# Block 0 of a retention and FFN layer: constants on another queue, and another order of copies, scan, variance products and weight sums

## The chip, the core and the metric

The kernel runs on one core of a Trainium2 chip. The metric is the device time in microseconds (us) from the start to the end of one execution. A core has five engines that run side by side: TensorE (PE, with its weight loads PEld), VectorE (DVE), ScalarE (ACT), GpSimd (POOL) and SyncE (SP). SP issues most transfers, ScalarE issues a few. Every engine works through its own instructions strictly in the order in which the program writes them, and waits at an instruction whose operands or whose buffer are not ready.

## What is computed

One layer of a small network over 4 sequences of 1024 tokens with 512 features, in float32:

```python
lam = clip(1 - 2**-beta, tiny, 1 - 1e-9)
def attn(x):                               # x: (4, 1024, 512), normalised
    q, v = heads(x @ Wq.T), heads(x @ Wv.T)          # 16 heads of 32
    ret = scan(v)                          # state = lam * state + v_t, along each sequence
    out = layernorm(q * ret) * gamma + beta_ln
    return (out * silu(x @ Wg.T)) @ Wo.T
def ffn(x):                                # weights rounded to float8_e4m3, kept in float32
    gate = silu((x @ r8(gate_w)) * gate_scale)       # 512 -> 1536
    return ((gate * ((x @ r8(up_w)) * up_scale)) @ r8(down_w)) * down_scale
x = x + norm(attn(norm(x)))                # norm: layernorm without weights, eps 1e-5
x = x + norm(ffn(norm(x)))
```

## The kernel before

**Tiles and blocks.** The 4096 tokens are cut into eight blocks of TB = 512 tokens, each of NS = 4 tiles of 128 tokens. Features lie in NC = 4 chunks of 128, the FFN's inner dimension in NI = 12 chunks. A `Retention` object does the attention part of a block, an `Ffn` object its FFN. In what follows, `a` is block 0, `b` block 1, `n` block 2, `f` the FFN of the running block, `l` that of the block before.

**The order of the work.** All instructions go through `InOrder`, so each engine executes them exactly as the program text calls them. There is no planner. Block 0's attention is written out by hand, mixed with the start of block 1's. Then a loop over t (blocks) and i (12 chunks of the FFN) follows: step i computes `f.gate(i)`, `f.up(i)` and `f.fuse(i)`, and `f.down(i - 2)`, and `if` lines place pieces of the next blocks between them. Step t = 0 also does block 1's attention and prepares block 2.

**The attention part.** Each tile is normalised (`norm_x`), transposed on TensorE (`turn_x`, into a PSUM bank) and copied out (`keep_x`) into the tile xnT. That tile exists once: block 1's copies have to wait until block 0's last product that reads it, `a.gate(3)`, is through. `v(c)`, `q(c)` and `gate(c)` are the products with the weights, per chunk of features. Their PSUM banks are named: two called "pf", two called "pa0" and "pa1", four called "pd0" to "pd3". `scan(c)` is the retention scan on VectorE and frees the bank of `v(c)`; `y_of(c)` is the product q * ret. `silu(c)` on ScalarE frees the bank of `gate(c)`. The normalisation of y goes over the features, that is over partitions: `mean` and `var` are products of a sum with a matrix of 1/512. `center_y` subtracts the mean and builds the squares' sum on ScalarE and POOL. `var` also issues the square root on ScalarE, whose functions need another table than silu's; `rstd_y` is the reciprocal of it on VectorE; `z(c)` scales y, applies gamma and beta and multiplies by the gate. In block 1, `halves` first splits a sum into two fp32r parts, on ScalarE and VectorE.

**The output part.** For each tile s: `o(s)` is the product with Wo, `o_moments(s)` its mean and rstd (statistics on VectorE, rstd on POOL), `x1_of(s)` normalises it on ScalarE and adds x on POOL, `x1_moments(s)` and `x1n_of(s)` normalise the sum. `turn_x1n(s)` transposes on TensorE. From block 1 on, `move_x1n(s)` does it instead with 32 x 32 transpositions on VectorE and five transfers through DRAM on SP. `upper_of(s)` on ScalarE and `rest_of(s)` on VectorE split the result into the two fp32r parts that the FFN's products read.

**Rounding of the FFN's weights.** Pieces of 128 x 1024 are loaded, and `rounds(n)` takes n steps of a generator on VectorE: a mask, an addition, a subtraction into the weight tile (which also frees a buffer, so that SP loads the next piece). `units()` issues two ScalarE operations for each open mask.

**Weight sums.** Blocks 2 to 7 compute v, q and g by seven products of half-sized matrices in place of eight. `weight_sums(k)` makes the sums of the quarters of a weight matrix in place with four VectorE operations of 128 x 512; `keep_sums` stores the four results in DRAM (four transfers on SP). In the loop at t = 0 this is done for v, q and g at i = 8, 9 and 10: the sums right before `f.gate(i)`, after `b.x1_moments(i - 8)`, the stores near the end of the step. `fetch_weights` loads a factor into the ring `w_ring`, which takes the place of Wv, four at i = 9. `t_sums` takes that of Wq and `mids` that of Wg, so their first writers wait for the stores of the sums. `n.product()` at i = 11 begins block 2's products: it copies the first result to `mids` on ScalarE, behind `b.upper_of(2)`.

**The start.** `load_x` sends half of each of block 0's tiles by SP and half by ScalarE. Then `load_const` issues the six constants on ScalarE's queue, and `load_square` the weights on SP's. Ahead of all of ScalarE's computing stands one Exp on a constant, which loads its table.

Of the kernel before, what the change touches and what calls it, by code (L numbers as in the profile page):

```python
# [23 lines left out]
def retention_ffn_sandwich(  # L24
# [64 lines left out]

    def load_const(src, cols, name):  # L90
        t = const.tile([P, cols], F32, tag=name, name=name)
        act.dma_start(t, src)
        return t
# [7 lines left out]

    beta_sb = load_const(beta, NC, "beta_sb")
    wv_sb = load_square(wvT, "wv_sb")
    wq_sb = load_square(wqT, "wq_sb")
    gamma_sb = load_const(gamma, NC, "gamma_sb")
    lnb_sb = load_const(lnb, NC, "lnb_sb")
    gs_sb = load_const(gate_s, NI, "gs_sb")
    us_sb = load_const(up_s, NI, "us_sb")
    ds_sb = load_const(down_s.to_broadcast([P, D]), D, "ds_sb")

# [104 lines left out]
    def units():  # L215

        while open_units:
            _, c = open_units.pop(0)
            act.activation(c, c, AF.Relu, bias=neg_low)
            act.activation(c, c, AF.Identity, scale=1.5 * 2.0**20, bias=low_unit)  # L220
# [123 lines left out]

    def weight_sums(k):

        src, w = squares[k]
        v = src.rearrange("(c p) f -> p c f", p=P)
        a11, a12, a21, a22 = (w[:, i : i + 2, o : o + H] for o in (0, H) for i in (0, 2))
        operands[k] = {1: v[:, 0:2, 0:H], 2: v[:, 2:4, 0:H], 4: v[:, 2:4, H:D]}  # L350
        dve.tensor_tensor(a22, a21, a22, ALU.add)
        dve.tensor_tensor(a21, a11, a21, ALU.subtract)
        dve.tensor_tensor(a11, a22, a11, ALU.subtract)
        dve.tensor_tensor(a12, a12, a11, ALU.subtract)
        return {5: a22, 7: a21, 6: a11, 3: a12}

    def keep_sums(k, done):
        for j, t in done.items():
            operands[k][j] = dram.tile([P, 2, H], F32, tag=f"sum_{k}{j}", name=f"dsum_{k}{j}", bufs=1)
            sp.dma_start(operands[k][j], t)  # L360
# [482 lines left out]
    wg_sb = load_square(wgT, "wg_sb")  # L843
    squares["g"] = wgT, wg_sb
    a = Retention(0, x_first)
    a.new_xnT()
# [57 lines left out]
    for s in range(NS):  # L904
        b.turn_x(s, f"pd{s}")
    a.var()
    a.rstd_y()
    a.silu(2)
# [4 lines left out]
    b.keep_x(3, dve.tensor_copy)  # L913
    a.silu(3)
    units()
    b.v(0, "pf", early)
    b.v(0, "pf", later)
    for c in range(NC):
        a.z(c)
    b.v(1, "pf")  # L920
    b.scan(0)
    b.v(2)
# [40 lines left out]
    a.rest_of(2)  # L963
    rounds(3, now=False)
    a.turn_x1n(3)
    a.upper_of(3)
    b.q(2, "pd0", early)
    units()
    a.rest_of(3)
    b.y_of(1)  # L970

# [4 lines left out]
    for t in range(NB):  # L976
        f, n = Ffn(a), None
        fast = b is not None and b.fast
        for i in range(NI):
# [29 lines left out]
            if b and not fast and i == 5:  # L1009
                b.z(0)  # L1010
            if b and i >= 8:
                b.x1_moments(i - 8)
            if t == 0 and 8 <= i < 11:
                done = weight_sums("vqg"[i - 8])
            f.gate(i)
# [31 lines left out]
            if b and not fast and i == 4:  # L1047
                b.halves()
                rounds(3, now=False)
                b.g_of(1)  # L1050
                b.var()
            if b and not fast and i == 5:
# [20 lines left out]
            units()  # L1073
            f.up(i)
            f.fuse(i)
            if t == 0 and i == 4:
# [55 lines left out]
            if b and n and i == 11:  # L1132
                b.rest_of(3)
            if t == 0 and 8 <= i < 11:
                keep_sums("vqg"[i - 8], done)

# [28 lines left out]
            if t == 0 and i == 9:  # L1165
                w_ring = wpool.tile([P, RING, 2, H], F32, tag="wv_sb", name="w_ring")
                for _ in range(RING):
                    fetch_weights()
# [78 lines left out]
```

## Time and profile before

| what | value |
|---|---|
| median of three runs | 985.41 us (984.66 to 985.66) |
| the profiled execution | 985.64 us, of it the span of the profile 983.8 us |
| from the start to the first FFN product | 95.2 us |
| from the start to the first FFN product of t = 1 | 204.6 us |
| TensorE busy, 0 to 98 us | 94.05 us |
| TensorE busy, 98 to 205 us | 102.23 us |
| TensorE busy, 205 to 984 us | 768.65 us |
| VectorE busy in the same stretches | 75.61, 86.58, 501.51 us |

The table divides the span at the start of block 0's FFN and at the start of t = 1. All edits lie in code that runs before 205 us. In the profile, each instruction stands under its engine with the tiles that it writes and reads: pv, pq, pg, po, pfg, pfu and pd are the products of v, q, gate, o and of the FFN; ptx and pt are transpositions, scr the pieces of weights, st and mv statistics, xs the transposed tile on its way to DRAM (mxs). Behind an instruction stands, in square brackets, how long its engine was idle before it and what ended the wait. SPq and ACTq are issues of transfers.

### The profile page before, as it was taken

The numbers are of one execution on the slowest core, as the hardware profiler recorded it, in microseconds if no ns is written. First come the engines' busy times: TensorE is split into PE (matmuls) and PEld (weight loads), VectorE is DVE, ScalarE is ACT, GpSimd is POOL, SyncE is SP. The second block draws the span as 40 slices with busy tenths as digits, with TensorE's granted clock in tenths as the row PEclk, the third lists the DMA queues.
The fourth block names the chain that finished last, engine by engine and source line by source line (L and its number), as shares of the span: only waits on it lengthen the run. The fifth ranks groups of instructions, "written<-read, shape, count | busy, mean of one in ns | idle before, by whom it ended". The sixth has DMA issues, their size and how long they took to land.

```text
span 983.8 us, 11259 instructions
## 1 busy us (share of the span) xinstructions
PE 964.9 (98%) x3950; PEld 735.9 (75%) x3950; DVE 663.7 (67%) x1019; ACT 369.6 (38%) x556; POOL 265.7 (27%) x346
## 2 busy tenths in 40 slices
PE   9999999999999999999999999999999999999996
PEld 7455766678876888678876788768887788867885
DVE  5996979656666567665686666766667765656535
ACT  3555565466645125221432215321152211522323
POOL 1405121422324033240513305133142312322020
PEclk9999999999999999999999999999999999999998
DMA  9311323752416426254242623245241552213021
GB/s 296 122 62 65 130 65 90 213 178 76 150 53 152 127 77 234 77 139 127 86 129 88 180 75 115 89 131 151 83 150 59 134 139 78 73 43 107 1 86 43
DMA packets 90936, 110.07 MB, mean 112 GB/s; under 512 B 8064, under 2 KB 55424, under 8 KB 90880
## 3 DMA queue, kind: packets, MB, share of 16 engines
q1 hardware_dynamic: 89296, 108.43, 36.9%
q10 hardware_dynamic: 1584, 0.94, 0.4%
q8 instruction: 31, 0.51, 0.2%
q14 instruction: 25, 0.20, 0.1%
HBM read 76.56 MB, written 32.77 MB: 111 GB/s over the span
## 4 chain that ended last, share of the span: by engine, by line
PE 82%; DVE 9%; ACT 4%; POOL 2%; issue 1%; DMA 1%; SPq 0%; ACTq 0%; DVEq 0%; POOLq 0%
PE pfu L74 15%; PE pfg L74 15%; PE pd L74 15%; PE pv L74 10%; PE pq L74 9%; PE pg L74 9%; PE po L74 8%; DVE st L74 2%; DVE scr L74 1%; POOL mv L74 1%; POOL x L74 1%; DVE fuse L74 1%; ACT x1n L74 1%; DVE gate L74 1%; DVE xs L74 1%
## 5 line engine op out<-in xcount | busy, mean ns | idle before, releaser
L74 PE MATMUL pfu<-x1nT,up_sb 128*128 128x512 f32 x768 | 212.5, 419 | 0.0
L74 PE MATMUL pfg<-x1nT,gate_sb 128*128 128x512 f32 x768 | 195.3, 396 | 0.4 <-DVE x1nT L74 0.4
L74 PE MATMUL pd<-down_sb,fuse 128*128 128x512 f32 x720 | 186.8, 401 | 0.0
L74 PEld LDWEIGHTS pfu<-x1nT,up_sb 128*128 128x128 f32 x768 | 145.1, 189 | 42.5 <-issue 12.9
L74 PEld LDWEIGHTS pfg<-x1nT,gate_sb 128*128 128x128 f32 x768 | 144.2, 188 | 30.4 <-DVE x1nT L74 0.8
L74 PEld LDWEIGHTS pd<-down_sb,fuse 128*128 128x128 f32 x720 | 135.3, 189 | 27.5
L74 ACT CAST fuse<-gate 128x512 fp32r<-128x512 f32 x90 | 55.7, 619 | 235.5 <-DVE gate L74 235.5
L74 ACT ACTIVATE gate<-pfg,gs_sb 128x512 f32<-128x512 f32 x96 | 65.7, 684 | 195.6 <-PE pfg L74 195.5
L74 DVE SCALAR_TENSOR_TENSOR gate<-pfu,us_sb,gate 128x512 f32<-128x512 f32 x96 | 71.8, 748 | 73.7 <-PE pfu L74 71.2
L74 PE MATMUL po<-wo_sb,y 128*128 128x512 f32 x256 | 114.5, 592 | 0.0
L74 POOL TENSOR_SCALAR mv<-mv 128x1 f32<-128x1 f32 (+1 forms) x82 | 19.4, 237 | 300.3 <-DVE mv L74 299.2
L74 PEld LDWEIGHTS po<-wo_sb,y 128*128 128x128 f32 x256 | 48.2, 189 | 50.3 <-issue 46.6
L74 DVE TENSOR_TENSOR fuse<-gate,fuse 128x512 fp32r<-128x512 f32 x90 | 75.0, 834 | 12.4 <-ACT fuse L74 12.4
L74 POOL TENSOR_TENSOR ysum<-y 128x256 f32<-128x256 f32 (+1 forms) x14 | 14.0, 998 | 190.3 <-DVE y L74 190.3
L74 POOL TENSOR_TENSOR x<-x,x1n 128x512 f32<-128x512 f32 x32 | 46.8, 1462 | 45.7 <-DVE x1n L74 36.7
L74 DVE BATCH_NORM_STATS2 st<-x 128x6 f32<-128x512 f32 x64 | 43.6, 681 | 13.8 <-POOL x L74 11.2
L74 POOL TENSOR_TENSOR mv<-mv,nhalf 128x1 f32<-128x1 f32 (+1 forms) x75 | 46.1, 615 | 6.2
L74 PE MATMUL pg<-t_sums,w_ring 128*128 128x256 f32 x192 | 45.7, 381 | 0.6 <-ACT mids L74 0.6
L74 PE MATMUL pv<-t_sums,w_ring 128*128 128x256 f32 x192 | 45.3, 379 | 0.0
L74 PE MATMUL pq<-t_sums,w_ring 128*128 128x256 f32 x192 | 45.3, 379 | 0.0
L74 PEld LDWEIGHTS pg<-t_sums,w_ring 128*128 128x128 f32 x192 | 35.9, 189 | 7.3 <-ACT mids L74 2.1
L74 PEld LDWEIGHTS pv<-t_sums,w_ring 128*128 128x128 f32 x192 | 36.3, 189 | 5.7
(150 smaller groups left out, 1336.8 us busy)
## 6 DMA issues: line engine op xcount, KB each, us to landing
kept<-x SPq DMA_DIRECT2D x32, 256.0 KB, 2.1
x<-kept SPq DMA_DIRECT2D x32, 256.0 KB, 3.7
x<-in_x SPq DMA_DIRECT2D x28, 256.0 KB, 4.3
out<-d SPq DMA_DIRECT2D x27, 256.0 KB, 2.1
xnT<-mx SPq DMA_DIRECT2D x24, 256.0 KB, 4.8
w_ring<-dsum_v SPq DMA_DIRECT2D x24, 256.0 KB, 2.7
w_ring<-dsum_q SPq DMA_DIRECT2D x24, 256.0 KB, 2.7
w_ring<-dsum_g SPq DMA_DIRECT2D x24, 256.0 KB, 2.6
```

Source lines behind the costliest of these rows:

```text
L74: return lambda *args, **kwargs: tc.keep_in_program_order(op(*args, **kwargs))
```

## The change

The diff has six parts.

1. The constants gamma, lnb, gs, us and ds are loaded on SP's queue after Wg, in place of ScalarE's queue at the start; beta stays on ScalarE's.
2. In block 0, `a.var()` and `a.rstd_y()` follow the copies `b.keep_x` and `a.silu(3)` in place of preceding `a.silu(2)`. `b.scan(0)` precedes `a.z` and `b.v(1)`.
3. Of the three rounding steps before `a.turn_x1n(3)`, the third moves behind `a.rest_of(3)`.
4. At i = 4, `b.var()` follows `f.up(4)` in place of `b.g_of(1)`.
5. The weight sums become a generator: four steps for v at i = 8, six at i = 9 (q's four and two of g), two at i = 10, these ahead of `b.x1_moments(2)`. g's stores follow them at once; v's and q's stay where they were.
6. Of the first four loads into the ring, two are issued at i = 9 and two at i = 10.

```diff
--- before.py
+++ after.py
@@ -87,9 +87,9 @@
 
     x_first = [load_x(0, s, [sp, act]) for s in range(NS)]
 
-    def load_const(src, cols, name):
+    def load_const(src, cols, name, queue=None):
         t = const.tile([P, cols], F32, tag=name, name=name)
-        act.dma_start(t, src)
+        (queue or sp).dma_start(t, src)
         return t
 
     def load_square(src, name):
@@ -99,14 +99,9 @@
             sp.dma_start(w[:, 2 * h : 2 * h + 2, :], v[:, 2 * h : 2 * h + 2, :])
         return w
 
-    beta_sb = load_const(beta, NC, "beta_sb")
+    beta_sb = load_const(beta, NC, "beta_sb", act)
     wv_sb = load_square(wvT, "wv_sb")
     wq_sb = load_square(wqT, "wq_sb")
-    gamma_sb = load_const(gamma, NC, "gamma_sb")
-    lnb_sb = load_const(lnb, NC, "lnb_sb")
-    gs_sb = load_const(gate_s, NI, "gs_sb")
-    us_sb = load_const(up_s, NI, "us_sb")
-    ds_sb = load_const(down_s.to_broadcast([P, D]), D, "ds_sb")
 
 
     gate_sb = wpool.tile([P, NC, I], F32R, tag="gate_sb", name="gate_sb")
@@ -342,20 +337,28 @@
     squares = {"v": (wvT, wv_sb), "q": (wqT, wq_sb)}
     operands = {}
 
-    def weight_sums(k):
-
-        src, w = squares[k]
-        v = src.rearrange("(c p) f -> p c f", p=P)
-        a11, a12, a21, a22 = (w[:, i : i + 2, o : o + H] for o in (0, H) for i in (0, 2))
-        operands[k] = {1: v[:, 0:2, 0:H], 2: v[:, 2:4, 0:H], 4: v[:, 2:4, H:D]}
-        dve.tensor_tensor(a22, a21, a22, ALU.add)
-        dve.tensor_tensor(a21, a11, a21, ALU.subtract)
-        dve.tensor_tensor(a11, a22, a11, ALU.subtract)
-        dve.tensor_tensor(a12, a12, a11, ALU.subtract)
-        return {5: a22, 7: a21, 6: a11, 3: a12}
-
-    def keep_sums(k, done):
-        for j, t in done.items():
+    def weight_sums():
+
+
+        for k, (src, w) in squares.items():
+            v = src.rearrange("(c p) f -> p c f", p=P)
+            a11, a12, a21, a22 = (w[:, i : i + 2, o : o + H] for o in (0, H) for i in (0, 2))
+            operands[k] = {1: v[:, 0:2, 0:H], 2: v[:, 2:4, 0:H], 4: v[:, 2:4, H:D]}
+            made[k] = {5: a22, 7: a21, 6: a11, 3: a12}
+            dve.tensor_tensor(a22, a21, a22, ALU.add)
+            yield
+            dve.tensor_tensor(a21, a11, a21, ALU.subtract)
+            yield
+            dve.tensor_tensor(a11, a22, a11, ALU.subtract)
+            yield
+            dve.tensor_tensor(a12, a12, a11, ALU.subtract)
+            yield
+
+    made = {}
+    adding = weight_sums()
+
+    def keep_sums(k):
+        for j, t in made[k].items():
             operands[k][j] = dram.tile([P, 2, H], F32, tag=f"sum_{k}{j}", name=f"dsum_{k}{j}", bufs=1)
             sp.dma_start(operands[k][j], t)
 
@@ -842,6 +845,11 @@
         load_piece(n)
     wg_sb = load_square(wgT, "wg_sb")
     squares["g"] = wgT, wg_sb
+    gamma_sb = load_const(gamma, NC, "gamma_sb")
+    lnb_sb = load_const(lnb, NC, "lnb_sb")
+    gs_sb = load_const(gate_s, NI, "gs_sb")
+    us_sb = load_const(up_s, NI, "us_sb")
+    ds_sb = load_const(down_s.to_broadcast([P, D]), D, "ds_sb")
     a = Retention(0, x_first)
     a.new_xnT()
     warm(14)
@@ -903,8 +911,6 @@
     b.new_xnT()
     for s in range(NS):
         b.turn_x(s, f"pd{s}")
-    a.var()
-    a.rstd_y()
     a.silu(2)
     a.gate(3, "pf")
     b.keep_x(0)
@@ -912,13 +918,15 @@
     b.keep_x(2, dve.tensor_copy)
     b.keep_x(3, dve.tensor_copy)
     a.silu(3)
+    a.var()
+    a.rstd_y()
     units()
     b.v(0, "pf", early)
     b.v(0, "pf", later)
+    b.scan(0)
     for c in range(NC):
         a.z(c)
     b.v(1, "pf")
-    b.scan(0)
     b.v(2)
     b.scan(1)
     rounds(3)
@@ -961,12 +969,13 @@
     a.rest_of(1)
     b.y_of(0)
     a.rest_of(2)
-    rounds(3, now=False)
+    rounds(2, now=False)
     a.turn_x1n(3)
     a.upper_of(3)
     b.q(2, "pd0", early)
     units()
     a.rest_of(3)
+    rounds(1, now=False)
     b.y_of(1)
 
 
@@ -1008,10 +1017,15 @@
                 n.shift()
             if b and not fast and i == 5:
                 b.z(0)
+            if t == 0 and i == 10:
+                for _ in range(2):
+                    next(adding)
+                keep_sums("g")
             if b and i >= 8:
                 b.x1_moments(i - 8)
-            if t == 0 and 8 <= i < 11:
-                done = weight_sums("vqg"[i - 8])
+            if t == 0 and i in (8, 9):
+                for _ in range(4 if i == 8 else 6):
+                    next(adding)
             f.gate(i)
             if t == 0 and i in (5, 6):
                 n.norm_x(2 * i - 10, True)
@@ -1048,7 +1062,6 @@
                 b.halves()
                 rounds(3, now=False)
                 b.g_of(1)
-                b.var()
             if b and not fast and i == 5:
                 b.g_of(2)
                 b.z(1)
@@ -1072,6 +1085,8 @@
                 n.input_sums(1, 2, 3, 4)
             units()
             f.up(i)
+            if t == 0 and i == 4:
+                b.var()
             f.fuse(i)
             if t == 0 and i == 4:
                 b.rstd_y()
@@ -1131,8 +1146,8 @@
                 n.fetch_x()
             if b and n and i == 11:
                 b.rest_of(3)
-            if t == 0 and 8 <= i < 11:
-                keep_sums("vqg"[i - 8], done)
+            if t == 0 and i in (8, 9):
+                keep_sums("vq"[i - 8])
 
             if i == f.lag:
                 f.sums()
@@ -1164,7 +1179,8 @@
                 n.stats(1)
             if t == 0 and i == 9:
                 w_ring = wpool.tile([P, RING, 2, H], F32, tag="wv_sb", name="w_ring")
-                for _ in range(RING):
+            if t == 0 and i in (9, 10):
+                for _ in range(RING // 2):
                     fetch_weights()
             if t == 0 and i == 10:
                 t_sums = wpool.tile([P, 4, 2, H], F32, tag="wq_sb", name="t_sums")
```

## The prediction, made before the changed kernel was run

> **What bounds the kernel now.** I read the page first, then TensorE's waits, then the chain of waits, then the engine timelines of the stretches that the diff touches. All times are microseconds from the start of the profiled execution, whose span is 983.8 of 985.64.
>
> ```profile
> PE 964.9 (98%) x3950; PEld 735.9 (75%) x3950; DVE 663.7 (67%) x1019; ACT 369.6 (38%) x556; POOL 265.7 (27%) x346
> ```
>
> TensorE is busy 98% of the span, so a change is worth at most what TensorE waits in the stretch it touches. Who it waits for up to 250 us:
>
> ```profile
> PE pt L74 <- ACT x1n L74: 2.3, 2, 2.0
> PE pv L74 <- ACT xnT L74: 2.3, 2, 1.2
> PE var L74 <- ACT half L74: 1.4, 1, 1.4
> PE pv L74 <- ACT mids L74: 1.1, 1, 1.1
> ...
> PE pfg L74 <- DVE x1nT L74: 0.4, 1, 0.4
> ```
>
> Columns are the total, the count and the longest. After 205 us there is only 0.8 us of such waits in 779 us, so a shift at the end of block 0 is the shift of the whole kernel. Each wait above has an edit on it: the two on xnT (at 9.95 and 56.97), the one on x1nT (96.19), var (130.43), and turn and mids (197.64, 202.97). If TensorE were all that counted, they would all be gains. The timelines say otherwise. VectorE (DVE) has no idle of note from 42.9 to 74.2, and what follows is a chain of single steps:
>
> ```profile
> 54.12 3.35 DVE L74 RECIPROCAL rstd<-rstd 128x512 f32<-128x512 f32 x1
> 57.38 1.22 DVE L74 COPY xnT<-ptx 128x512 f32<-128x512 f32 x2
> ...
> 74.46 0.70 DVE L74 BATCH_NORM_STATS2 st<-po 128x6 f32<-128x512 f32 x1 [0.28 <-PE po L74]
> ```
>
> The reader is to see that at 74.46, where o_moments(0) starts, VectorE has 0.28 us of slack. From there the chain of waits goes statistics, POOL, ScalarE, POOL's addition, four times at 3.38 us per tile (POOL's additions start at 78.38, 81.77, 85.16, 88.55), and ends in the transposition of tile 3 at 93.21, for which TensorE waits. A later start at 74.46 is a later FFN. ScalarE (ACT) just before:
>
> ```profile
> 50.22 1.28 ACT L74 ACT_TABLE_LOAD   x1
> 52.41 0.69 ACT L74 ACTIVATE rstd<-var,eps_sb 128x512 f32<-128x512 f32 x1 [0.91 <-PE var L74]
> 53.11 1.28 ACT L74 ACT_TABLE_LOAD   x1
> 54.41 0.60 ACT L74 ACTIVATE g<-pg 128x512 f32<-128x512 f32 x1
> 55.84 1.07 ACT L74 COPY xnT<-ptx 128x512 f32<-128x512 f32 x2 [0.84 <-PE pg L74]
> ```
>
> Now the root is ready at 53.1, before VectorE wants it at 54.12: the reciprocal runs while TensorE does gate(3) (to 54.96) and b's copies wait for it, since both blocks share the tile xnT.
>
> **What the Trainium skill says.** ScalarE: Activation LUTs, "What ACT_TABLE_LOAD costs", gives about 1283 ns for a load, and its section on table sets says that cheap functions lie in every set; the trace agrees (1.28 us, and no load between the root at 132.19 and the Relu after it). DMA: Bandwidth & Descriptors, "Issuing engines are not separate DMA queues": moving an issue saves the sequencer's time alone; here five issues take 0.33 + 0.44 + 0.33 + 0.33 + 0.44 = 1.9 us of ScalarE's queue. GPSIMD Engine Reference, "Key points": POOL shares its SBUF interfaces with VectorE; beside the weights' additions POOL's two steps of a rstd take 0.54 + 1.00 us (186.26), alone 0.19 + 0.55 (195.59). TensorE: Matmul & The Clock Gate, Part 1: after an idle window the clock is halved for a window of about 3.4 us; the trace shows 0.50 granted in 132 to 134, after the wait for var.
>
> **Part 1, constants.** ScalarE's queue is held by its issues until 7.41, then come the table load (7.44), lam (8.74) and the copies (8.85 to 9.90); TensorE waits until 9.95. With beta alone on it the queue is free at 3.9 and the load ends near 5.2, so the copies follow the transpositions: the second ends at 8.41, its copy near 9.0, TensorE starts at 9.05. Gain 0.9; at least 0.5, if the second half of wv, issued at 5.7 and landing 3.7 to 4.4 later, is late for the fifth product. SP issues the five after wg, ahead of b's x (needed at 37.6) and wo (needed at 71): some 2 us of SP's queue, covered by over 15 us. wq no longer stands behind them. TensorE has no gap from 9.95 to 55.8, and VectorE follows it, so both carry the 0.9.
>
> **Part 2, var after the copies.** In the times of before: gate(3) ends at 54.96; ScalarE copies tiles 0 and 1 until 56.07, VectorE 2 and 3 until 56.15. The var product fills 54.96 to 55.8, so b.v(0) starts at 56.1 instead of 56.97: TensorE gains 0.8. But the root now stands behind silu(3) (to 56.6) and a table load (to 57.9) and ends at 58.55. VectorE waits from 54.2 to 54.96 and from 56.15 to 58.55, 3.2 us that it did not wait before. Behind the reciprocal stand all its work: scan(0) 1.4, z 5.9, scan(1) 1.4, rounds 3.0, scan(2), rounds and scan(3) 3.9. It reaches o_moments(0) at about 77.5 instead of 74.46: +3.0, bounds 2.0 and 3.6 (the root waits less, or the copies longer). The scan put first frees the bank for b.v(3) in time, so no further wait comes of it. TensorE's 0.8 is lost in front of turn(0): o(3) ends earlier, x1n comes later.
>
> **Part 3, rounds 2 + 1.** rest_of(3) waited for an addition and a subtraction until 95.45; now it follows upper_of(3), 94.5 to 95.1, before TensorE ends q(2) at 95.24. The first FFN group effectively began at 95.96 (seven products from 96.19, one of 0.23 done), so the gain is 0.7. VectorE is no earlier, but it has 0.33 and 1.02 us of waiting for pfu (101.74, 108.81), which take up the difference. Shift at 109: −0.9 + 3.0 − 0.7 = +1.4.
>
> **Part 4, b.var after up(4).** TensorE no longer waits 1.4 us, and may escape the halved window. But the root again goes behind: after silu g at 130.9, units() waits for the mask of 131.6 and holds ScalarE until 133.95, the table load until 135.2, the root until 135.95. The reciprocal starts at 136.0 instead of 135.40: +0.6 (bounds 0 and +1). The chain of waits runs through that reciprocal: scr, rest(4), the load at 142.36, silu(5), scr, VectorE at 148.48, then VectorE without idle to 170. z(3) ends at 155.73 and TensorE reaches o(0) at 156.35, so TensorE's gain ends in waits for silu(5) and y.
>
> **Part 5, additions.**
>
> ```profile
> 176.78 2.83 DVE L74 TENSOR_TENSOR wq_sb<-wq_sb 128x512 f32<-128x512 f32 x4
> 179.79 0.71 DVE L74 STREAM_TRANSPOSE xs<-x1n 128x512 f32<-128x512 f32 x1 [0.17 <-ACT x1n L74]
> ...
> 185.26 0.69 DVE L74 BATCH_NORM_STATS2 st<-x 128x6 f32<-128x512 f32 x1 [1.35 <-POOL x L74]
> ```
>
> Six of 0.71 instead of four at i=9: the transposition slips by 1.3. At i=10 two (1.4 us) stand ahead of the statistics, in idle time of 1.35, and POOL's rstd behind them runs alone: −0.8. x1n(3), which TensorE awaits at 197.64, comes +0.5 (to +1.1 if POOL's addition is slowed). On SP, dsum_g's four issues (2.9 us) now stand before the transposed tile's:
>
> ```profile
> 191.16 1.88 SPq L74 DMA_DIRECT2D mxs<-xs  x4
> 195.52 0.34 SPq L74 DMA_DIRECT2D x1n<-mxs  x1
> ```
>
> These go to about 194.2 and 198.6, upper_of(2) on ScalarE from 198.35 to 201.4, and behind it stand the cast of fuse and the copy to mids, at 202.45. Now that copy waits for dsum_g until 202.33. One wait replaces the other: +0.1 at 202.97, bounds −0.7 and +0.8. Two ring loads a step later are in time (j=2 lands near 202, needed at 203).
>
> **Sum.** −0.9 + 3.0 − 0.7 + 0.6 + 0.1 = +2.1 us; 985.64 + 2.1 = 987.7. The profiled execution lies 0.23 over the median of the runs, 985.41, so this is 0.23% over that median. A measurement of this kernel can tell about 0.2% from no change: 983.4 to 987.4.
>
> **Rivals.** Forecast, reciprocal's delay carried through, 987.7: for it VectorE's missing idle; against it that 0.3 us less is already within the bound. Chance 0.50, of it 0.35 slower and 0.15 same; its own range 986.4 to 989.0.
> A clock window on top: new waits in front of turn(0) (2.4 us) and at silu(5) halve the clock once, 1.7 us lost as at 132 to 135: 989.4. Against it, 2.05 us of waiting at 197 brought none. 0.17, slower.
> Slack takes up the delay, the other side: the one mechanism is the x1 chain of 74 to 93, which would have to run below 3.38 us per tile with its po ready early. Then 3.0 falls to 0: 985.64 − 0.9 = 984.7. It decides once it recovers over 0.4 of the 3.0. Against it, POOL's fixed order. 0.22, of it 0.20 same and 0.02 faster.
> TensorE's gaps are the bound after all: 0.9 + 0.8 + 0.7 + 3.1 (var and the halved window) + 0.7 (mids) = 6.2, 979.4. Against it, the chain of waits on other engines. 0.11, of it 0.09 faster and 0.02 same.
> Faster 0.11, same 0.37, slower 0.52. Range 984.0 to 990.3: it holds the first three and leaves out the last and the worst of the second.
>
> **What would show it.** TensorE's first v at 9.0; a reciprocal at about 57.6 with over 2 us of VectorE idle before it; o_moments(0) near 76.6; TensorE waiting over 2 us at turn(0); FFN about 97; VectorE waiting for the root at i=4; SP's mxs after dsum_g. Wrong if o_moments(0) isn't later, or if the root ends by 56.

## The result

| | median | runs | ratio to before, 95% interval |
|---|---|---|---|
| before | 985.39 us | 6, 984.66 to 985.68 | |
| after | 989.76 us | 6, 987.88 to 990.83 | 1.0043 [1.003, 1.0056] |

The changed kernel is 4.4 us slower. The sign and the range of the prediction held; its size, +2.1 us, is half of what was measured, and the forecast's own range, 986.4 to 989.0, was missed by 0.8. Three of the executions that follow were slow ones (1095.82 to 2035.05 us) and are left out of every median. The profiled execution of after took 990.15 us, of it a span of 988.3 us, 4.5 us more than that of before. The page of after, engines and their busy time:

```profile
PE 968.1 (98%) x3950; PEld 737.0 (75%) x3950; DVE 663.7 (67%) x1019; ACT 369.7 (37%) x556; POOL 264.7 (27%) x346
```

The work is the same: the counts are equal, and VectorE's busy time is 663.7 us in both. TensorE's busy time rose by 3.2 us with no product added, so something slowed its clock; more on that below. TensorE's waits up to 260 us in after (waited for by whom, total, times, longest):

```profile
PE pt L74 <- ACT x1n L74: 4.8, 3, 2.4
PE pfg L74 <- ACT gate L74: 2.7, 1, 2.7
...
PE pv L74 <- ACT xnT L74: 0.5, 2, 0.3
PE mu L74 <- DVE half L74: 0.5, 1, 0.5
PE pv L74 <- DMA wv_sb<-in_wvT: 0.4, 1, 0.4
```

Against before, the waits for xnT fell from 2.3 to 0.5, and those for half at var (1.4) and mids in front of pv (1.1) are gone. In their place stand 2.7 us for silu(5), which writes the gate, 2.5 more for x1n, 0.5 for half at mu, and 0.4 for the second half of wv. Of the waits that the edits were laid against, only the one for x1n has not gone or shrunk, and the kernel is slower.

Where the time came from shows in the start of the same instruction in both profiled executions:

| step | before | after | difference |
|---|---|---|---|
| o_moments(0) on VectorE | 74.46 | 76.69 | +2.23 |
| first FFN group (before: its effective start, as in the prediction) | 95.96 | 97.89 | +1.93 |
| reciprocal of b, i = 4 | 135.40 | 138.60 | +3.20 |
| first o of b | 156.35 | 160.01 | +3.66 |
| statistics of x(0), i = 8 | 166.65 | 170.28 | +3.63 |
| statistics of x(2), i = 10 | 185.26 | 190.82 | +5.56 |
| transposition of x1n(3) | 197.64 | 202.38 | +4.74 |
| first FFN product of t = 1 | 204.62 | 209.50 | +4.88 |

So the first 76 us lose 2.2, the FFN's pieces up to the reciprocal another 1.3, and the way of the last tiles, from i = 8 to the transposition, about 1.1. Each column is one execution, and two of them can differ at such a point without any edit: in the five kernels whose code is that of before up to o_moments(0), it starts between 74.12 and 74.91. First the stretch in which the prediction put the largest term. VectorE in after (start, duration, instruction, idle before it and what ended it):

```profile
54.46 1.29 DVE L74 COPY xnT<-ptx 128x512 f32<-128x512 f32 x2 [0.77 <-PE pg L74]
58.07 3.35 DVE L74 RECIPROCAL rstd<-rstd 128x512 f32<-128x512 f32 x1 [2.32 <-ACT rstd L74]
...
76.69 0.69 DVE L74 BATCH_NORM_STATS2 st<-po 128x6 f32<-128x512 f32 x1
```

and ScalarE in front of that reciprocal, in after:

```profile
54.46 1.07 ACT L74 COPY xnT<-ptx 128x512 f32<-128x512 f32 x2 [4.30 <-PE pg L74]
55.42 0.61 ACT L74 ACTIVATE g<-pg 128x512 f32<-128x512 f32 x1
56.06 1.28 ACT L74 ACT_TABLE_LOAD   x1
57.35 0.69 ACT L74 ACTIVATE rstd<-var,eps_sb 128x512 f32<-128x512 f32 x1
```

VectorE stands idle for 0.77 + 2.32 us where it had no idle before, because copy, silu, table load and root now lie in one row on ScalarE in front of its reciprocal. From there to 76.69 VectorE has no idle, so nothing takes the delay up.

At i = 4 the same pattern recurs. ScalarE in after:

```profile
134.22 1.15 ACT L74 ACTIVATE scr<-scr,neg_low 128x1024 f32<-128x1024 f32 x1 [0.87 <-DVE scr L74]
135.41 1.16 ACT L74 ACTIVATE scr<-scr,low_unit 128x1024 f32<-128x1024 f32 x1
136.58 1.28 ACT L74 ACT_TABLE_LOAD   x1
137.88 0.69 ACT L74 ACTIVATE rstd<-var,eps_sb 128x512 f32<-128x512 f32 x1
```

The root waits behind the two steps of a piece of weights, which in turn waited 0.87 us for VectorE's mask; the reciprocal at 138.60 then waits 1.35 us for the root. And the clock that TensorE was granted, by stretches of after (stretch, length, busy us and instructions of PE, PEld, DVE, ACT, POOL, granted clock, share of DMA, GB/s):

```profile
86.00:88.00 2.00, 2.00 (x4) 0.81 (x4) 0.95 (x3) 1.60 (x5) 1.52 (x4) 0.55 0.35 131
88.00:90.00 2.00, 2.00 (x4) 0.86 (x3) 1.21 (x3) 1.72 (x5) 1.59 (x4) 0.60 0.25 93
...
148.00:150.00 2.00, 2.00 (x6) 1.52 (x6) 1.65 (x3) 2.00 (x4) 0.00 (x0) 0.50 0.01 5
...
202.00:204.00 2.00, 1.62 (x6) 1.53 (x7) 0.00 (x0) 0.32 (x1) 1.92 (x3) 0.56 0.25 26
```

Three windows at about half clock follow three waits: 2.1 us in front of the transposition at 85.45 and 2.7 for silu(5), both new, and 2.4 in front of the one at 202.38, which had 2.05 before. This is the rival "a clock window on top" in full sight, three times over. From this profile alone, two accounts fit the missing 2.3 us: a part cost more than its term (theory A), or the clock did (theory B). The experiments were made to tell these apart.

### The profile page after: what moved, and what is told of

It is laid out like the page before. It is cut to its first block, busy times and chain, and to the rows that moved or that the text cites. A ratio compares the mean times of both kernels' runs of the same rounds, so it can differ in the third digit from the quotient of the medians.

```text
span 988.3 us, 11263 instructions
## 1 busy us (share of the span) xinstructions
PE 968.1 (98%) x3950; PEld 737.0 (75%) x3950; DVE 663.7 (67%) x1019; ACT 369.7 (37%) x556; POOL 264.7 (27%) x346
## 4 chain that ended last, share of the span: by engine, by line
PE 83%; DVE 9%; ACT 4%; POOL 2%; issue 1%; DMA 1%; SPq 0%; ACTq 0%; DVEq 0%; POOLq 0%
PE pfg L74 16%; PE pfu L74 15%; PE pd L74 15%; PE pq L74 10%; PE pg L74 9%; PE pv L74 8%; PE po L74 8%; DVE st L74 1%; DVE scr L74 1%; POOL mv L74 1%; DVE y L74 1%; ACT x1n L74 1%; DVE fuse L74 1%; PE pt L74 1%; DVE gate L74 1%
```

## The experiments

Times are medians, against runs of the kernel before on the same chip. The parts carry the numbers of the change.

### Each part alone

**Part 1**, the constants' loads and nothing else:

```diff
-        act.dma_start(t, src)
+        (queue or sp).dma_start(t, src)
...
-    beta_sb = load_const(beta, NC, "beta_sb")
+    beta_sb = load_const(beta, NC, "beta_sb", act)
...
-    gamma_sb = load_const(gamma, NC, "gamma_sb")
...
     wg_sb = load_square(wgT, "wg_sb")
     squares["g"] = wgT, wg_sb
+    gamma_sb = load_const(gamma, NC, "gamma_sb")
...
```

> The kernel before with part 1 alone (constants on SP after Wg, beta on ScalarE). Chain theory: in the changed kernel TensorE is 0.5 us ahead at 12 us (second half of wv lands late), and no later wait of before is bound to a fixed time, so the whole kernel gains 0.5 us: o_moments(0) at 74.0, total about 984.9. Rival (clock theory: the 4.4 us come from halved-clock windows behind TensorE's waits, the order of work matters little): also near -0.5, no new wait. Wrong for both if it is above +0.2.

Measured 984.73 against 985.21, ratio 0.9992 [0.9984, 1.0]: −0.48, half of the prediction's 0.9, which the interval still holds. TensorE's first products of v in after:

```profile
8.79 1.13 PE L74 MATMUL pv<-xnT,wv_sb 128*128 128x256 f32 x4 [0.23 <-ACT xnT L74]
10.30 1.13 PE L74 MATMUL pv<-xnT,wv_sb 128*128 128x256 f32 x4 [0.38 <-DMA wv_sb<-in_wvT]
```

TensorE starts 1.16 us earlier (9.95 before), does four products and then waits 0.38 for the second half of wv. This is not the rule: of the seven traces with part 1, only this one and the one without part 2 have such a wait. With part 1 alone, TensorE starts at 9.24 and does its eight products in a row. It then starts behind the transpositions of x, and their own start varies: 6.13 in after, 7.16 with the clock kept (below). The second group of v starts at 12.32 to 13.11 in six traces without part 1 (mean 12.70) and at 11.65 to 12.73 in the seven with it (mean 12.26). So the gain is about 0.4 us on the mean, and the next limit was the transposition or the load, whichever came later.

**Part 2**, var and the scan:

```diff
-    a.var()
-    a.rstd_y()
     a.silu(2)
...
     a.silu(3)
+    a.var()
+    a.rstd_y()
     units()
...
+    b.scan(0)
     for c in range(NC):
         a.z(c)
     b.v(1, "pf")
-    b.scan(0)
```

> Part 2 alone (var and rstd_y after the copies and silu(3), scan(0) ahead of z). Chain theory: the root ends at 57.9 + 0.5 = 58.4, VectorE idles 0.8 + 2.3 us, o_moments(0) comes 2.7 us later than in before (77.2), the FFN starts 2.7 later (VectorE still ends rounds(3) before rest_of(3)), and at the end of block 0 the kernel is 2 to 3 us slower: 987.4 to 988.4, with up to 0.7 more where the clock is halved behind the wait for turn(0). Clock theory: o_moments(0) may be later, but the FFN's start is taken up by TensorE's 0.8 us gain; slower only as far as a 0.5 clock shows behind turn(0), so under +1.

Measured 988.09 against 985.21, ratio 1.0025 [1.0017, 1.0034]: +2.88. VectorE of this kernel:

```profile
54.98 1.29 DVE L74 COPY xnT<-ptx 128x512 f32<-128x512 f32 x2 [0.77 <-PE pg L74]
58.59 3.35 DVE L74 RECIPROCAL rstd<-rstd 128x512 f32<-128x512 f32 x1 [2.32 <-ACT rstd L74]
```

The same two idles as in after, 3.09 us; o_moments(0) starts at 77.21, 2.75 later than before. TensorE's clock is at about half from 86 to 90 in this execution, and again from 134 to 138.

**Part 3**, the rounding steps:

```diff
-    rounds(3, now=False)
+    rounds(2, now=False)
     a.turn_x1n(3)
...
     a.rest_of(3)
+    rounds(1, now=False)
```

> Part 3 alone (two rounding steps ahead of rest_of(3), one behind). Chain theory: rest_of(3) follows upper_of(3) at once, the FFN's first group runs without its gap, 0.7 us earlier, and VectorE's waits for pfu at 101.7 and 108.8 take up the later rounds: the whole kernel gains 0.5 to 0.8 us. Theory that VectorE's own work is the bound from 90 to 122: no gain, since its sum of work is unchanged; reciprocal at i=4 no earlier, total within 0.2.

Measured 984.98 against 985.15, ratio 0.9999 [0.9991, 1.0007]: −0.17, no difference that can be told: the expected gain of 0.5 to 0.8 failed, and its rival, VectorE's own work as the bound, fits better. FFN does start earlier: 20.79 us after o_moments(0) where before it was 21.50. The gain is lost in the next 25 us. VectorE of this kernel, the masks of the first two pieces of weights:

```profile
101.85 1.40 DVE L74 TENSOR_SCALAR scr<-scr 128x1024 int32<-128x1024 int32 x1
...
108.49 1.14 DVE L74 TENSOR_SCALAR scr<-scr 128x1024 int32<-128x1024 int32 x1
```

and what POOL does beside them:

```profile
101.42 1.28 POOL L74 TENSOR_TENSOR ysum<-ysum,y 128x512 f32<-128x512 f32 x1 [3.09 <-DVE y L74]
...
107.79 1.29 POOL L74 TENSOR_TENSOR ysum<-ysum,y 128x512 f32<-128x512 f32 x1 [5.08 <-DVE y L74]
```

With part 1 alone, VectorE's same two masks and POOL's two additions are

```profile
101.82 1.00 DVE L74 TENSOR_SCALAR scr<-scr 128x1024 int32<-128x1024 int32 x1
...
108.89 0.68 DVE L74 TENSOR_SCALAR scr<-scr 128x1024 int32<-128x1024 int32 x1
...
100.97 1.29 POOL L74 TENSOR_TENSOR ysum<-ysum,y 128x512 f32<-128x512 f32 x1 [3.08 <-DVE y L74]
...
107.35 1.29 POOL L74 TENSOR_TENSOR ysum<-ysum,y 128x512 f32<-128x512 f32 x1 [5.08 <-DVE y L74]
```

that is 0.40 and 0.46 us less for the masks. What moved is the distance to POOL's addition: VectorE waits for pfu 0 and 0.17 us in place of 0.32 and 1.02, so that its masks start 0.43 and 0.70 us after the addition does; with part 1 alone they start 0.85 and 1.54 us behind it, the second one after the addition's end. At the second mask VectorE is 0.67 us ahead of part 1 alone (34.37 us after o_moments(0) against 35.04), at the next instruction 0.21, and the reciprocal of i = 4 keeps just that: 60.03 against 60.24. So it is the second mask's 0.46 that counts; the first one's 0.40 is taken up by the wait for pfu behind it. No run takes the addition away, but the traces together leave little doubt (the last section): every mask that starts during such an addition ends 0.54 to 0.57 us after the addition does.

**Part 4**, b.var:

```diff
                 b.g_of(1)
-                b.var()
...
             units()
             f.up(i)
+            if t == 0 and i == 4:
+                b.var()
             f.fuse(i)
```

> Part 4 alone (b.var after up(4), behind units() on ScalarE). Chain theory: reciprocal at i=4 0.6 to 0.7 us later than 135.40, TensorE ahead by 3 us at pd, then waiting 2.7 us for silu(5) in front of gate(6); o(0) 0.6 later, plus up to 0.4 if the clock is halved after that wait: total +0.5 to +1.0. Clock theory: TensorE no longer waits at var and its halved window at 132 goes, so the kernel gains 1 to 3 us unless the wait at gate(6) halves the clock again.

Measured 986.80 against 985.21, ratio 1.0017 [1.001, 1.0023]: +1.59, where the prediction's step had +0.6 with 1 as its upper bound, and +0.5 to +1.0 was expected here. ScalarE and VectorE of this kernel:

```profile
132.05 1.15 ACT L74 ACTIVATE scr<-scr,neg_low 128x1024 f32<-128x1024 f32 x1 [0.86 <-DVE scr L74]
...
134.41 1.28 ACT L74 ACT_TABLE_LOAD   x1
135.71 0.69 ACT L74 ACTIVATE rstd<-var,eps_sb 128x512 f32<-128x512 f32 x1
...
136.43 3.35 DVE L74 RECIPROCAL rstd<-rstd 128x512 f32<-128x512 f32 x1 [1.35 <-ACT rstd L74]
```

The reciprocal starts at 136.43, 61.66 us after o_moments(0). Before it was 60.94, so by the profile of before the price is 0.7. But before's 60.94 is not typical. In its profiled execution the clock stood at 0.50 from 132 to 134, and that lies inside the interval; with part 1 alone it did not (columns as in the windows of after, first before, then part 1 alone):

```profile
132.00:134.00 2.00, 2.00 (x6) 1.59 (x5) 1.97 (x2) 1.96 (x4) 0.00 (x0) 0.50 0.00 0
...
132.00:134.00 2.00, 2.00 (x10) 1.65 (x10) 1.97 (x3) 1.97 (x3) 0.00 (x0) 1.00 0.00 0
```

Part 1 and parts 5 and 6 alone leave this stretch as it was and show 60.24 and 60.22; part 3 alone, which changes its beginning, shows 60.03, and the version that beats both, below, 60.05. All four have the same 1.4 us wait for var and no halved window there. Only before and part 2 alone have one behind that wait, and the latter shows 61.73. Against 60.24 the price is 1.4.

**Parts 5 and 6**, the sums and the ring:

```diff
-            if t == 0 and 8 <= i < 11:
-                done = weight_sums("vqg"[i - 8])
+            if t == 0 and i in (8, 9):
+                for _ in range(4 if i == 8 else 6):
+                    next(adding)
...
+            if t == 0 and i == 10:
+                for _ in range(2):
+                    next(adding)
+                keep_sums("g")
             if b and i >= 8:
                 b.x1_moments(i - 8)
...
-                for _ in range(RING):
+            if t == 0 and i in (9, 10):
+                for _ in range(RING // 2):
                     fetch_weights()
```

> Parts 5 and 6 alone (sums 4, 6 and 2, g's first, ring loads 2 and 2). Chain theory: statistics of x(2) 1.9 us later, of x(3) 1.1 later, turn of tile 3 at 198.7 instead of 197.64; mids is copied behind upper_of(2), which waits for the transfer that now stands behind dsum_g; first product of t=1 0.5 to 1.2 us later: total +0.5 to +1.2. Clock theory: the wait for turn of tile 3 grows beyond 2 us, so the loss shows as a halved window there (about 1 us) and without it the kernel is no slower than before.

Measured 985.62 against 985.21, ratio 1.0 [0.9992, 1.0008]: +0.41, not told from zero and under the +0.5 to +1.2 expected. The transposition of x1n(3) comes 123.56 us after o_moments(0), 122.47 with part 1 alone: +1.1, the upper bound of the step. One cause can be read in VectorE's line for the two sums at i = 10. In after, two such sums without POOL beside them take 1.41 us (at 183.17):

```profile
184.61 2.39 DVE L74 TENSOR_TENSOR wg_sb<-wg_sb 128x512 f32<-128x512 f32 x2
```

POOL's addition beside them takes 1.70 us in place of 1.27, the condition that the prediction gave for +1.1. At the first FFN product of t = 1 nothing of it is left to see (129.17 us after o_moments(0); before 130.16, part 1 alone 129.67).

**What follows from the five.** −0.48 + 2.88 − 0.17 + 1.59 + 0.41 = +4.23, and all together cost +4.37. By the ratios the five are −0.8, +2.5, −0.1, +1.7 and 0.0 us, +3.3 together, and the whole is +4.2; each part is known to within 0.6 to 0.8 us, the sum to within about 1.7 (if the errors are independent), the whole to within 1.3. So the parts add up as far as can be told, and nothing needs to come on top; an item of about 1 us that needs all of them at once is not excluded. To see it from the other side, everything but part 2:

> The changed kernel with part 2 undone (var and rstd_y ahead of silu(2), scan(0) behind v(1)). If part 2's delay of VectorE is the largest term and the parts add up, o_moments(0) returns to 74.0 and the total falls by 2.9 to about 986.9, still 1.3 to 1.7 over before (part 4 and its clock window). If the parts only cost together, it falls to before or stays near 989.

Measured 986.71 against 985.24, ratio 1.001 [1.0003, 1.0016]: +1.47. The four parts alone add to +1.35, and after less part 2 gives 4.37 − 2.88 = +1.49.

### Why part 4 costs 1.6

Part 4 with the root one place earlier, behind f.up(4) but ahead of units(). `f.up` has only TensorE's products and `units` only ScalarE's steps, so their exchange alone changes no engine's order:

```diff
-            units()
             f.up(i)
             if t == 0 and i == 4:
                 b.var()
+            units()
             f.fuse(i)
```

> As part 4, but b.var() ahead of units(), so that the table load and the root precede the two scr operations on ScalarE. If what part 4 costs is the root's place behind units(), the reciprocal at i=4 follows fuse(4) at about 134.7 (part 4: 136.4) and VectorE does not wait for the root; total within 0.5 of before, that is about 1.2 us below part 4 alone (986.8). If it costs by the later product itself or by the clock halved in front of gate(6), it stays near 986.8, with the same 0.5 window at 146 to 150.

Measured 984.78 against 985.15, ratio 0.9995 [0.9987, 1.0003]: −0.37, so 2.0 less than part 4 as it is. ScalarE and VectorE of this kernel:

```profile
130.70 1.28 ACT L74 ACT_TABLE_LOAD   x1
132.00 0.69 ACT L74 ACTIVATE rstd<-var,eps_sb 128x512 f32<-128x512 f32 x1
...
134.48 3.34 DVE L74 RECIPROCAL rstd<-rstd 128x512 f32<-128x512 f32 x1
```

The root ends at 132.7, the reciprocal starts at 134.48 without waiting (60.23 us after o_moments(0)), and TensorE waits for silu(5) 1.29 us in place of 2.73; no halved window follows. So the price of part 4 is the order on ScalarE: not that var was late on TensorE, but that the root was put behind 2.3 us of weights and a wait for a mask. In the traces the 2.0 is the reciprocal's 1.4 and a second loss behind it: in part 4 alone the wait for silu(5) is followed by the clock at half:

```profile
146.00:148.00 2.00, 2.00 (x6) 1.59 (x5) 1.48 (x3) 2.00 (x4) 0.00 (x0) 0.51 0.01 4
```

and by i = 8 the delay has grown from 1.4 to 1.9 us (93.41 after o_moments(0), against 91.47 with part 1 alone).

### Is the clock an item of its own?

The changed kernel, with products that nothing uses filling TensorE's three long waits:

```diff
+    def keep_clock(name, home, n):
+        turn_ = pa_turn[0]
+        z = ps_tile(name, home)
+        for _ in range(n):
+            pe.matmul(z[:, :P], mean_w, mean_w, start=True, stop=True)
+        pa_turn[0] = turn_
...
+    keep_clock("kc0", "pf", 9)
     a.turn_x1n(0)
...
+            if t == 0 and i == 6:
+                keep_clock("kc1", f"pa{1 - pa_turn[0]}", 11)
             f.gate(i)
...
+                if t == 0:
+                    keep_clock("kc2", "pa1", 10)
                 b.turn_x1n(3, "pf")
```

A first kernel had 18, 22 and 18 products, and the last line without its condition:

> The changed kernel with dummy products of two constants (18, 22 and 18, some 2 us each) in front of turn_x1n(0), of gate at i=6 and of turn_x1n(3) at i=11, where TensorE waits 2.1, 2.7 and 2.4 us; the outputs do not depend on them. If the halved clock behind these waits makes the rest of the loss over the chains (0.4 + 0.4 + 1.0), the trace shows 1.00 at 86 to 90, 146 to 152 and 202 to 206, and the time falls by 1.2 to 1.8 us to about 988.2. If the clock costs nothing beyond the waits, it stays at 989.8; if the dummies get in the way, it rises.

Measured 1009.99 against 985.15, ratio 1.0247 [1.0234, 1.0261]. A miss of the experiment, and not of the theory: each product is two instructions of 0.116 us in the trace, so that the fillers lasted 4.2 to 5.1 us instead of 2, and the last stood in every block. The time says nothing of the clock. With 9, 11 and 10 products, in block 0 alone:

> The changed kernel with dummy products (9, 11 and 10, at 0.23 us each 2.1, 2.6 and 2.3 us) in block 0 only, in front of turn_x1n(0), of gate at i=6 and of the last turn_x1n at i=11; the outputs do not depend on them. If the halved clock behind the three waits costs time over the chains, the trace shows no 0.5 window at 86 to 90, 146 to 152 and 202 to 206, and the time falls from 989.8 by 0.8 to 1.8 us. If the sum of the parts alone (-0.5, +2.9, -0.2, +1.6, +0.4 = +4.2) is the cause and the clock takes nothing beyond them, it stays within 0.4 of 989.8.

Measured 989.47 against 985.24, ratio 1.0045 [1.0032, 1.0057], the same as after. The same kernel again, for a trace of its usual course:

> The kernel of e9_clock_kept_2 once more, for its trace. Theory that the parts' sum is the cause: the clock is 1.00 at 86 to 90, 146 to 152 and 202 to 206, the FFN still starts 21.2 us after o_moments(0), as in the changed kernel, and the time is within 0.4 of 989.8. If halved windows are still there, the dummies did not keep the clock and the question of their price stays open.

Measured 990.39 against 985.69, ratio 1.0056 [1.0042, 1.007]. The stretches that were halved, in this kernel:

```profile
86.00:88.00 2.00, 2.00 (x8) 1.08 (x8) 1.32 (x4) 1.28 (x4) 1.51 (x4) 1.00 0.35 131
88.00:90.00 2.00, 2.00 (x8) 0.96 (x7) 0.82 (x3) 1.70 (x5) 1.78 (x3) 1.00 0.06 22
...
148.00:150.00 2.00, 2.00 (x8) 1.33 (x8) 1.30 (x3) 2.00 (x3) 0.00 (x0) 1.00 0.01 4
...
202.00:204.00 2.00, 2.00 (x12) 1.66 (x11) 0.00 (x0) 0.00 (x0) 2.00 (x2) 1.00 0.34 54
```

The clock is at 1.00 in all three, the first FFN group comes 20.48 us after o_moments(0) in place of 21.20, the statistics of x(0) 92.43 in place of 93.59. Yet the kernel is as slow as after. By the first FFN product of t = 1 half of the 1.2 us gained is lost (132.22 us after o_moments(0), 132.81 in after), in a new wait on TensorE of this kernel:

```profile
207.68 1.97 PE L74 MATMUL pv<-xnT,w_ring 128*128 128x256 f32 x8 [1.82 <-DMA w_ring<-in_wvT]
```

This is the ring load of j = 2, which part 6 issues a step later. So theory B falls as an item of 2.3 us on top: without halved windows there is no gain in the total that can be told, where 2.3 us could be. It also isn't nil: 0.7 us of the delay at FFN and 1.2 at i = 8 (the second includes the first) were windows. They belong to the measured price of parts 2 and 4, whose own traces have them (at 86 to 90 and 146 to 150), and the last one hides a late load.

Every run, profiled or not, also has its mean granted clock on record, and this bears on what windows are worth in a total. The six runs of after fall into two groups: three at 0.993 took 990.13, 990.15 and 990.83 us, three at 0.997 and 0.998 took 989.34, 989.39 and 987.88. So some 0.8 us goes with the lower clock. But the two at 0.997 are still 4.3 to 4.7 us above the runs of before at that clock (medians of 984.64 to 985.08 on four chips). This compares runs that fell out one way or the other and not a setting that was made; it agrees with the fillers, which put the kernel at 989.47 and 990.39 and not at 987.7.

### A version that beats both

Parts 1 and 3, and in place of parts 4 to 6 one move: SP's four stores of g's sums go between the four outward transfers of move_x1n(2) and the one back.

```diff
-        sp.dma_start(dst, m)
+        if between:
+            between()
+        sp.dma_start(dst, m)
...
-                b.move_x1n(i - 8)
+                b.move_x1n(i - 8, (lambda: keep_sums("g", done)) if t == 0 and i == 10 else None)
...
-            if t == 0 and 8 <= i < 11:
+            if t == 0 and i in (8, 9):
                 keep_sums("vqg"[i - 8], done)
```

> The kernel before with parts 1 and 3, and with g's stores put between the two halves of the last tile's way through DRAM at i=10 (after its four transfers out, ahead of the one back), sums as in before. Chain theory: -0.6 (part 1), -0.6 (part 3), and TensorE's wait for mids at 203 (1.1 us) goes, as dsum_g lands 3 us earlier, while upper_of(2) comes at most 0.5 later: about -2 us, 983.2. Rival: mids only swaps waits (as part 5 does), then -1.2, 984.0.

Measured 983.61 against 985.15, ratio 0.9983 [0.9976, 0.9989]: 1.5 us faster than before, and some 6 us faster than after. SP's queue of this kernel:

```profile
190.01 1.86 SPq L74 DMA_DIRECT2D mxs<-xs  x4
192.11 2.56 SPq L74 DMA_DIRECT2D dsum_g<-wg_sb  x4
194.92 0.45 SPq L74 DMA_DIRECT2D x1n<-mxs  x1
```

The transfer back has to wait for the outward ones anyway; the stores fill that time. The tile is out first, as before, and ScalarE reads it back at 198.26 (198.35 before); the copy to mids is at 199.30 (202.33 before), and the wait for mids of 1.1 us is gone. The first FFN product of t = 1 comes 127.85 us after o_moments(0), against 129.67 and 129.69 with part 1 and part 3 alone. The move was not run alone: that most of the gain over those two parts' −0.65 is its own is read from these traces. To this, the place of b.var from the experiment on part 4 was added:

> e8's kernel with b.var() also after up(4) and ahead of units(), as in e6. Chain theory: reciprocal at i=4 in the same place as in a run of before without a halved window (VectorE's own order sets it), so no gain beyond the window that the wait at var can bring: 983.0 to 983.9, against 983.6 for e8. Rival (TensorE's wait of 1.4 us at var is worth its length): 982.2.

Measured 984.20 against 985.24, ratio 0.9986 [0.9979, 0.9992]: no more than without it. TensorE's wait of 1.4 us for var, removed at no cost to the root, is worth nothing that can be told: it comes back as 1.29 us in front of the next gate product, and the reciprocal comes 60.05 us after o_moments(0) in both kernels, because VectorE's own row of work sets that stretch and not TensorE.

## Why the prediction was right, and where it was half the size

- **Part 2** (predicted +3.0): right, +2.88. The idles predicted were 0.76 and 2.4 us, found 0.77 and 2.32. That o_moments(0), set at 76.6, came at 76.69 is in part luck: its delay was 2.75 in place of 3.0, part 1 took off 0.4 less than counted, and one execution can be 0.4 off either way. The rival "slack takes up the delay" needed an x1 chain that recovers; POOL's additions come at 80.60, 84.00, 87.39 and 90.78, still one in 3.39 us. It falls, but for 0.3 us: with the clock kept, FFN starts 20.48 us after o_moments(0), and 20.78 to 20.79 in the four kernels with part 3 and without part 2.
- **Part 1** (−0.9, bound 0.5): the bound, −0.48. The late second half of wv, named as the condition of the bound, came true in two traces of seven; in four of the others the transpositions of x came later than in before's one execution, from which the 9.05 was worked out. In the sum I took the better end.
- **Part 3** (−0.7): mis-sized. The FFN's start is 0.7 earlier, as said. "VectorE is no earlier, but it has 0.33 and 1.02 us of waiting for pfu (101.74, 108.81), which take up the difference" held only to the second mask, where VectorE is 0.67 us ahead. The step that failed is to let that difference run on: with the waiting gone, this mask starts during POOL's addition and lengthens by 0.46 us, and mu then waits 0.5 us for half. What remains is −0.17, within what can't be told from zero. I had priced the moved step, and not what removing a wait does to the overlap of two other engines. The sharing of SBUF between POOL and VectorE was in the prediction, but used for POOL's small steps alone.
- **Part 4** (+0.6, at most +1): mis-sized, +1.59, the largest error and the only one clear of noise. The mechanism was right: the root behind units(), the reciprocal waiting, TensorE's gain ending in a wait for silu(5). The step that failed is "136.0 instead of 135.40: +0.6": the 136.0 was right (61.54 us after o_moments(0), measured 61.66), but the 135.40 carried a halved window that four of the six traces with this wait don't have, so that the subtraction set an undisturbed estimate against a disturbed reading. The prediction itself named the window ("0.50 granted in 132 to 134"), and I counted its going as TensorE's possible gain, not as something inside my own reference. To that comes the window after silu(5), about 0.5 in its trace.
- **Parts 5 and 6** (+0.1, −0.7 to +0.8): +0.41 by the total, within its bounds and within what can't be told from zero. x1n(3) slipped by the upper bound, 1.1. In after, the four stores of dsum_g stand before mxs on SP (194.57, 197.43), and ScalarE waits 2.97 us for the tile at upper_of(2), a late return as predicted. "Two ring loads a step later are in time" was argued with the times of before; in after, the load of j = 2 is issued at 203.11, behind SP's wait for mxs. In the run with the clock kept it is issued at 203.10, and TensorE waits 1.82 us for it, until 207.68.
- **The rival "a clock window on top"**, 989.4, is the nearest to the measured 989.76, and it is not the cause as I gave it: two of the three windows came where it said, but within the price of parts 2 and 4, and taking all three away brought nothing in the total; even after's own runs at a high clock, 989.34 and 989.39, keep nearly all of the loss. That its number fits is luck. **"TensorE's gaps are the bound"** falls plainly: some 4 us of the waits it counts were removed, and the kernel is slower; and where one of them was removed without delaying the root, in the experiment on a better version, nothing was gained.

The missing 2.3 us are then: part 4 1.0, part 3 0.5, part 1 0.4, parts 5 and 6 0.3, part 2 −0.1; together 2.1, and 0.1 of the sum of the five to the whole. Of these only part 4's is clear of noise: its interval, +1.0 to +2.3, leaves out +0.6, and the intervals of the others hold the predicted values. For parts 1, 3, 5 and 6 the traces named above are the better evidence.

## What to carry to other kernels

When an engine shows no idle behind an instruction that waits for a short result (here a reciprocal behind a root), keep the producer of that result ahead of everything else on its queue; here, filling TensorE's gap by delaying the producer bought nothing and cost the whole delay. Before subtracting two times, look whether the reference stretch holds a halved clock window or another accident of that one execution, best by a second execution. And time that a queue must spend waiting for its own transfer (SP between the tile's way out and back) was here a place for other stores, at no cost that shows.

## What was not expected of the hardware

- A VectorE mask of 128x1024 takes 0.68 us alone and 1.40 beside POOL's addition of 128x512, twice the time; two sums of 128x512 take 1.41 us alone and 2.36 beside it, and POOL's addition then 1.67 in place of 1.27. They wait for each other and don't slow each other. In twelve traces up to 220 us (all but the first two with fillers), 144 single masks clear of POOL's operations of 128x512 took 0.63 to 0.69 us; 30 that start during one took 0.99 to 1.77, and each ends 0.54 to 0.57 after POOL's operation does, however long they overlap; 24 that start before one took 0.68 or 0.69. So the one that starts first goes through, and a shift of 0.4 us decides which it is. The Trainium skill (VectorE: DVE Perf Modes, "Mode 2×_2P") says that an operation with a single tensor can take both read ports and so run at two elements a cycle, which an operation of two tensors can't. The trace agrees as far as it goes: undisturbed, the mask (one tensor) takes 0.68 us, the addition of 128x1024 behind it (two tensors) 1.22. Beside POOL the mask isn't merely as slow as an operation of two tensors: it takes up to 1.77.
- Waits of 2.1 (at 85.45), 2.7 and 2.4 us in after were each followed by a window at about half clock, and 1.4 us in before too; waits of 2.05 us (at 197.64 in before) and of 1.4 us (at var with part 1 alone) were not. At the transposition of x1n(3), the wait was 2.47 us with part 1 alone, and 198 to 200 stood at 0.50; with part 3 alone it was 2.49 us, and they stood at 1.00. The Trainium skill (TensorE: Matmul & The Clock Gate, Part 1) names at least one idle window of about 3.4 us as the condition, and says that the windows run freely. No wait here is that long, and the length of a wait alone doesn't say whether the clock halves. That the place of the wait against the windows decides would fit the differences between executions; no run here shows it.
- A product of 128x128 in float32 appears as two instructions of 0.116 us each: 18 of them are listed as 36 and took 4.18 us.
